# A last layer's loads moved from ScalarE's queue to SyncE's, and filler products tied to the statistics

## The chip, the cores and the metric

The kernel runs on one core of one Trainium2 chip. It is written in a tile framework in which a planner orders most instructions by its own costs and inserts the waits; in blocks marked as a manual schedule, the instructions of the named engines (of all engines, if none is named) keep the order in which they are written. The metric is device time in microseconds. Three runs of the kernel before took 3638.68, 3646.11 and 3650.18 us; the median is 3646.11.

## The reference

A tensor of 48 channels and 256 x 256 pixels passes through two layers, each with a residual. Layer 0 is an attention over 4 x 4 patches; layer 1 multiplies 64 x 64 windows by small matrices over width, height and channels. Cut to what matters:

```python
def _gn(v, G=16, eps=1e-5):            # group norm: 16 groups of 3 channels
    ...
    return ((g - m) / jnp.sqrt(s + eps)).reshape(v.shape)

def _L0_conv_ref(x, w_qkv, w_dw, temperature, w_proj):
    qkv = dwconv3x3(jnp.einsum('bchw,oc->bohw', x, w_qkv), w_dw)
    ...                                # heads, patches with a border, l2 norm
    attn = jax.nn.softmax(jnp.einsum('bhcn,bhcm->bhnm', q, k) * temperature, axis=-1)
    out = jnp.einsum('bhcn,bhnm->bhcm', v, attn)
    ...
    return jnp.einsum('bchw,oc->bohw', fold(out), w_proj)

def _L1_conv_ref(x, Ws, Hs, Cs, window_size):
    xb = x.reshape(B, C, H // ws, ws, W // ws, ws)
    return jnp.einsum('bcphqw,twW,thH,tcC->bCpHqW', xb, Ws, Hs, Cs).reshape(B, C, H, W)

x = x + _L0_conv_ref(_gn(x), ...)
x = x + _L1_conv_ref(_gn(x), Ws, Hs, Cs, 64)
```

## The kernel before

Layer 0 fills the first 3235 us and isn't touched. What follows is in two parts.

**Projection and statistics (L771 to L856).** Sixteen rows of pixels at a time, for both halves of the image, TensorE multiplies the attention's output by the projection (pps, L796), VectorE adds it to the pixels (L803) and takes the statistics of each 512 of them (bn_stats into st1, L807: 64 entries), and GpSimd stores the sum to x1s in DRAM (L812). The last step is done in two parts of 8 rows. SyncE then loads the first five pieces of x1s (L813 to L815). group_stats (L127) turns st1 into a mean and a reciprocal root in a short ping-pong between VectorE, TensorE and ScalarE, and the result is folded into the channel matrix csn (L849 to L855). In this block TensorE alone has a manual order: occupy(7) puts seven products without use ahead of the chain (identity by a tile nmx of zeros or row maxima, 256 columns, into a PSUM tile busy that nobody reads), and one more behind each small product of the chain.

**The last layer (L859 to L1014).** Its units are the 4 x 2 window rows and halves: yw is one of four bands of 64 image rows, xh the left or right 128 columns. For each unit over_c multiplies 32 rows of both window halves by csn (pa, L916), in 12 groups (4 pieces of 8 rows, each in groups of 3, 3 and 2 rows), and copies each group into zt (lzt, L924 to L928): VectorE mostly, ScalarE one group in four (one in two in the first unit). zt is laid out with the row index innermost, so that a copy in the order of pa steps 64 elements (256 bytes) at each element. over_w (pb, L942) multiplies by the width matrices, once for each of three t, and ScalarE copies the result into parts (lyt, L949). over_h (pc, L961) multiplies by the height matrices and sums over t; residual adds x1 (lrt, L975) and GpSimd stores to the output (L982). pa has two PSUM buffers, pb and pc one each; lyt and lzt have two SBUF buffers each.

**The order.** This part has a manual schedule on all engines. Unit u's over_w and over_h are interleaved with unit u + 1's over_c: for each of three channel groups q and each t, one over_w, then for t < 2 two groups of the next over_c, then, for t = 2, the over_h of the q before.

**The loads.** The inputs of later units come from x1s: rows (load_rows, L872, 64 x 4 rows of 1 KB, for the residual) and pieces (load_piece, L766, 48 channels x 4 rows, 4 KB runs, for over_c). rows_later and piece_later only put them in a list; begin_load (L899) takes the first of the list and issues it, after each over_w and each over_c group. They are issued from ScalarE's queue, which also holds ScalarE's copies, in program order. There are 44 of each kind.

Of the kernel before, what the change touches and what calls it, by code (L numbers as in the profile page):

```python
# [20 lines left out]
KS = 4  # L21
# [24 lines left out]
def conv_preact_kernel(  # L46
# [719 lines left out]
    def load_piece(yw, i, s, y, n, eng):  # L766

        y0 = yw * WS + s * HW + i * PR + y
        eng.dma_start(out=piece(yw, i)[s * 64 : s * 64 + C, y : y + n, :], in_=x1s[:, y0 : y0 + n, :])

    with tc.tile_pool(name="pj", bufs=3) as pj, tc.tile_pool(name="pjs", bufs=1) as pjs, tc.tile_pool(  # L771
        name="pps", bufs=3, space=PSUM
    ) as pps, tc.tile_pool(name="pp1", bufs=1, space=PSUM) as pp1:
        st1 = pjs.tile([P2, HALF * W // 512, 6], F32, name="st1")
        ov = os_.rearrange("t (c k) n -> t c k n", k=KK)
        for t in range(HALF // RP):
            ot = pj.tile([P2, KK, NP], F32, name="pot")
            xt = xts[t] if t < NX else pj.tile([P2, RP, W], F32, name="pxt")
            for s in range(2):
                r = slice(s * C, (s + 1) * C)  # L780
                y0 = s * HALF + t * RP
                nc.sync.dma_start(out=ot[r], in_=ov[s * (NT // 2 // TP) + t])
                if t >= NX:
                    nc.sync.dma_start(out=xt[r], in_=xc[:, y0 : y0 + RP, :])

            np = 2 if t + 1 == HALF // RP else 1
            R = RP // np
            for part in range(np):
                ys = slice(part * R, (part + 1) * R)
                n = R // KS * PX  # L790
                xv = xt[:, ys].rearrange("p (py ki) (px kj) -> p ki kj py px", ki=KS, kj=KS)
                for ki in range(KS):
                    ps = pps.tile([P2, KS, n], F32, name="pps")
# [24 lines left out]
        nc.gpsimd.memset(csn, 0.0)  # L818
        for s in range(2):
            nc.scalar.dma_start(  # L820
                out=csn[s * 64 : s * 64 + C].rearrange("c (t d) -> c t d", t=T3), in_=Cs.rearrange("t c d -> c t d")
            )
        at = pjs.tile([C, 64 + CK], F32, name="at")
        nc.gpsimd.memset(at, 0.0)
        for o in (C, 64 + C):
            nc.gpsimd.memset(at[:, o : o + 1], 1.0)
        gm2 = pjs.tile([P2, 64 + CK], F32, name="gm2")
        nc.vector.memset(gm2, 0.0)
        for o in (0, 64):
            nc.vector.tensor_copy(gm2[:, o : o + C], gm[:, 0:C])  # L830
        busy = pps.tile([P2, KS, 128], F32, name="pps")

        def occupy(n):

            for _ in range(n):
                nc.tensor.matmul(busy[:, 0:2, :], lhsT=ident[:, :P2], rhs=nmx, start=True, stop=True)

        with tc.manual_schedule(engines={mybir.EngineType.PE}):
            occupy(7)
            mv1, e1 = group_stats(st1, mean1, rstd1, pjs, pp1, lambda: occupy(1))  # L840
            pc1 = pp1.tile([64 + CK, 1], F32, name="pc1", tag="pstat")
            nc.tensor.matmul(pc1, lhsT=gm2, rhs=e1, start=True, stop=True)
            occupy(1)
            rstd2 = pjs.tile([64 + CK, 1], F32, name="rstd2")
            nc.vector.tensor_scalar_add(rstd2, pc1, EPS)
            nc.scalar.activation(rstd2, rstd2, AF.Sqrt)
            nc.vector.reciprocal(rstd2, rstd2)

            nc.vector.tensor_scalar_mul(csn, csn, rstd2)  # L849
            mcol = pjs.tile([C, 64 + CK], F32, name="mcol")  # L850
            nc.vector.tensor_scalar_mul(mcol, at, mean1[0:C])
            pb1 = pp1.tile([64 + CK, T3 * C], F32, name="pb1")
            nc.tensor.matmul(pb1, lhsT=mcol, rhs=csn[0:C], start=True, stop=True)
            occupy(1)
            nc.vector.tensor_sub(csn, csn, pb1)  # L855
    early.close()  # L856

# [1 line left out]
    with tc.tile_pool(name="lz", bufs=2) as lz, tc.tile_pool(name="lr", bufs=6) as lr, tc.tile_pool(name="ly", bufs=2) as ly, tc.tile_pool(name="ps1", bufs=2, space=PSUM) as ps1, tc.tile_pool(  # L859
# [20 lines left out]
            )  # L880

        loads = []

        def rows_later(yw, q):

            if yw < H // WS:
                for s in range(2):
                    for c in (0, 4):
                        loads.append(lambda s=s, c=c: load_rows(yw, q, s, c, 4, nc.scalar))

        def piece_later(n):

            yw, i = divmod(n, NPC)
            if yw < H // WS:
                for s in range(2):
                    for y in range(0, PR, PR // 2):
                        loads.append(lambda s=s, y=y: load_piece(yw, i, s, y, PR // 2, nc.scalar))

        def begin_load():  # L899

            if loads:
                loads.pop(0)()

        def over_c(u):

            yw, xh = units[u]
            zt = zts[u] = lz.tile([128, T3 * C, WS], F32, name="lzt")
            zv = zt.rearrange("p k (s y) -> p s y k", s=2)
            for p in range(NPC):
                xq = piece(yw, p)  # L910
                for g, (y0, n) in enumerate(((0, 3), (3, 3), (6, 2))):
                    pa = ps1.tile([128, 2, 512], F32, name="pa")
                    for i in range(n):
                        for s in range(2):
                            r = slice(s * 64, s * 64 + CK)
                            nc.tensor.matmul(  # L916
                                pa[:, s, i * T3 * C : (i + 1) * T3 * C],
                                lhsT=xq[r, y0 + i, xh * 128 : (xh + 1) * 128],
                                rhs=csn[r],
                                start=True,  # L920
                                stop=True,
                            )
                    y = p * PR + y0
                    to, src = zv[:, :, y : y + n, :], pa[:, :, : n * T3 * C].rearrange("p s (y k) -> p s y k", y=n)  # L924
                    if (p * 3 + g) % (4 if u else 2) == 1:
                        nc.scalar.copy(to, src)
                    else:
                        nc.vector.tensor_copy(to, src)  # L928
                    if xh and g == 2:
                        piece_later(yw * NPC + p + len(pieces))  # L930
                    yield

        def over_w(u, q, t):

# [54 lines left out]
        with tc.manual_schedule():  # L989
# [7 lines left out]
            for u in range(NU):  # L997
                yw, xh = units[u]
                ahead = over_c(u + 1) if u + 1 < NU else iter(())
                for q in range(NQ):  # L1000
                    if xh == 1:
                        rows_later(yw + 1, q)
                    parts[u, q] = ly.tile([128, T3, 1024], F32, name="lyt")
                    for t in range(T3):
                        over_w(u, q, t)
                        begin_load()
                        if t < 2:
                            for _ in range(2):
                                next(ahead, None)
                                begin_load()  # L1010
                        elif late:
                            over_h(*late)
                    late = u, q
# [42 lines left out]
```

## Time and profile before

| quantity | value |
|---|---|
| median of 3 runs | 3646.11 us (3638.68 to 3650.18) |
| the profiled execution | 3654.33 us, span 3652.5 us |
| TensorE products, busy | 3426.0 us (94%) |
| VectorE, ScalarE, GpSimd busy | 2115.9, 1898.0, 531.6 us |
| mean granted TensorE clock | 0.974 |
| first product of the last layer (pa) | 3380.54 us |
| last residual add | 3644.59 us |

PE is TensorE, PEld its weight loads, DVE VectorE, ACT ScalarE, POOL GpSimd, SP SyncE; ACTq and SPq are the queues of an engine where it issues transfers. A line of the timeline gives start, duration, engine, code line and operation, and in brackets how long the engine had been idle and what ended that. Matrix products of float32 run in two passes, so one product is two records. A line of stretches gives the busy time of each engine in the stretch, then TensorE's granted clock as a share of full speed, the DMA engines' busy share, and GB/s.

### The profile page before, as it was taken

To read this page: it belongs to the slowest core of one execution; us is meant where nothing else is said; L and a number is where in the kernel's file an instruction comes from. 1 tells how busy PE (TensorE), PEld (TensorE's weight loads), DVE (VectorE), ACT (ScalarE), POOL (GpSimd) and SP (SyncE) were. 2 spreads that over 40 slices of the span, in tenths; PEclk is the share of its full clock that TensorE was granted. 3 is DMA by queue.
4 is the path that set the end of the run, shared out by engine and by line. 5 is a ranking of instruction groups with operands and counts; after the bars stand their busy time and mean duration, and the time that the engine had idled before them with its cause. 6 is when DMAs were issued, how large, how long until landed. Compare 5 with 4: busy or idle time off the path is not lost.

```text
span 3652.5 us, 104961 instructions
## 1 busy us (share of the span) xinstructions
PE 3426.0 (94%) x46578; PEld 2874.1 (79%) x46578; DVE 2115.9 (58%) x3505; ACT 1898.0 (52%) x2699; POOL 531.6 (15%) x616
## 2 busy tenths in 40 slices
PE   2878999999999999999999999999999999976888
PEld 1337777888888888889888888888889888842765
DVE  5464775269727962796289528952894222257454
ACT  0245666566646664665466546654665444410343
POOL 2030121012201220122112111211121100010001
PEclk9988999999999999999999999999999999987899
DMA  7455665533323332333233323332333221059564
GB/s 159 157 125 146 169 183 154 172 92 97 91 74 87 95 86 74 86 93 94 73 82 98 90 81 82 93 86 81 82 93 92 62 54 28 19 141 283 119 156 107
DMA packets 241972, 386.78 MB, mean 106 GB/s; under 512 B 78130, under 2 KB 175778, under 8 KB 237000
## 3 DMA queue, kind: packets, MB, share of 16 engines
q1 hardware_dynamic: 187974, 244.77, 24.0%
q0 software_dynamic: 35264, 106.40, 12.8%
q10 hardware_dynamic: 18274, 28.83, 3.4%
q8 instruction: 368, 6.03, 0.7%
q14 instruction: 92, 0.75, 0.1%
HBM read 234.76 MB, written 144.90 MB: 104 GB/s over the span
## 4 chain that ended last, share of the span: by engine, by line
PE 81%; DMA 4%; DVE 3%; issue 2%; ACT 1%; SPq 1%; ACTq 0%; POOL 0%; POOLq 0%; DVEq 0%
PE big L339 37%; PE big L603 36%; PE pc L961 2%; PE pb L942 2%; PE pa L916 2%; PE big L179 1%; DVE acc L230 1%; PE pt L620 1%; DMA pxt<-in_x_dram 1%; DMA pad<-t 1%; PE pn L249 1%; DMA xs<-in_x_dram 1%; PE pst L557 1%; DVE xt L803 1%; DVE lzt L928 0%
## 5 line engine op out<-in xcount | busy, mean ns | idle before, releaser
L574 ACT ACTIVATE e<-big,nmx 128x1024 f32<-128x1024 f32 x1024 | 1143.9, 1117 | 878.0 <-PE big L339 617.8
L339 PE MATMUL big<-kt,qt 128*128 128x512 f32 x6144 | 1439.9, 393 | 31.9 <-DMA qt<-qkv 21.7
L603 PEld LDWEIGHTS big<-vn,e 128*64 128x64 f32 x32768 | 1358.7, 137 | 57.1 <-ACT e L574 30.6
L603 PE MATMUL big<-vn,e 128*64 128x96 f32 x32768 | 1389.1, 247 | 5.9 <-DVE oacc L614 2.4
L339 PEld LDWEIGHTS big<-kt,qt 128*128 128x128 f32 x6144 | 1148.4, 189 | 279.2 <-issue 29.3
L614 DVE TENSOR_TENSOR oacc<-big,oacc 128x768 f32<-128x768 f32 x480 | 453.4, 954 | 703.7 <-PE big L603 703.7
L230 DVE SCALAR_TENSOR_TENSOR acc<-pad,dwt,acc 126x1024 f32<-126x1024 f32 x592 | 765.6, 1293 | 39.7 <-ACT acc L211 23.9
L587 DVE TENSOR_REDUCE zt<-zs 128x1 f32<-128x4 f32 x256 | 38.5, 150 | 338.7 <-ACT e L574 338.7
L297 POOL DMA_DIRECT2D qkv<-o x72 | 52.8, 734 | 1247.6 <-ACT o L281 1247.6
L291 POOL TENSOR_TENSOR ol<-o,oh 126x1024 fp32r<-126x1024 f32 x78 | 184.7, 2368 | 311.7 <-DVE ss L245 238.4
L574 ACT ACTIVATION_READ_ACCUMULATOR e<-big,nmx 128x1 f32 x1024 | 196.2, 192 | 0.0
L281 ACT COPY o<-acc 126x1024 f32<-126x1024 f32 x74 | 158.8, 2146 | 0.0
L928 DVE COPY lzt<-pa 128x864 f32<-128x864 f32 (+1 forms) x69 | 101.2, 1507 | 69.2 <-PE pa L916 69.2
L949 ACT COPY lyt<-pb 128x1024 f32<-128x1024 f32 x69 | 70.7, 1025 | 116.3 <-PE pb L942 96.9
L241 ACT ACTIVATE sq<-acc 126x1024 f32<-126x1024 f32 x74 | 78.2, 1057 | 101.2 <-DVE acc L230 101.2
L796 PE MATMUL pps<-pot,wp 96*96 96x512 f32 x128 | 77.5, 770 | 56.2 <-DMA pot<-os__70 45.1
L182 ACT ACTIVATE ot<-big,bias 108x1024 f32<-108x1024 f32 x64 | 68.3, 1111 | 113.5 <-PE big L179 76.4
L211 ACT ACTIVATE acc<-pad,dwt 126x1024 f32<-126x1024 f32 x74 | 84.1, 1137 | 81.9 <-DMA pad<-t 81.9
L245 DVE TENSOR_REDUCE ss<-sq 126x64 f32<-126x1024 f32 x80 | 97.5, 1219 | 27.0 <-ACT sq L241 27.0
L942 PEld LDWEIGHTS pb<-wsb,lzt 64*64 64x64 f32 x4608 | 82.2, 140 | 37.2 <-issue 23.4
L219 PE MATMUL dps<-pad,diag 126*126 126x512 f32 x216 | 96.3, 606 | 15.5 <-DMA pad<-t 15.5
L796 PEld LDWEIGHTS pps<-pot,wp 96*96 96x96 f32 x128 | 26.0, 212 | 107.0 <-issue 73.8
(134 smaller groups left out, 2006.8 us busy)
## 6 DMA issues: line engine op xcount, KB each, us to landing
pad<-t SPq DMA_DIRECT2D x238, 254.0 KB
t<-ot SPq DMA_DIRECT2D x128, 217.7 KB
qkv<-ol POOLq DMA_DIRECT2D x78, 336.0 KB, 6.5
qkv<-oh POOLq DMA_DIRECT2D x70, 336.0 KB, 5.7
qt<-qkv SPq DMA_DIRECT2D x176, 96.0 KB
xs<-in_x_dram SPq DMA_DIRECT2D x128, 96.0 KB
os__70<-oo POOLq DMA_DIRECT2D x128, 96.0 KB, 2.1
pot<-os__70 SPq DMA_DIRECT2D x16, 768.0 KB
```

The source lines that it names most:

```text
L219: nc.tensor.matmul(ps[:, i, :], lhsT=diag[:, tap, :], rhs=self.pad[:, y : y + 2, dx : dx + W], start=(tap == 0), stop=(tap == 8),)
L230: nc.vector.scalar_tensor_tensor(self.acc, self.pad[:, dy : dy + KS, dx : dx + W], dwt[:, self.h, tap : tap + 1], self.acc, ALU.mult, ALU.add,
L245: nc.vector.tensor_reduce(self.ss, self.sq.rearrange("p a (x b) -> p x a b", b=KS), AX.XY, ALU.add)
L281: nc.scalar.copy(self.o.rearrange("p (a b) x -> p a b x", a=KS), self.acc.rearrange("p a (x b) -> p a b x", b=KS))
L291: eng.tensor_sub(self.ol, self.o, self.oh.bitcast(F32))
L339: nc.tensor.matmul(ps[:, i, :], lhsT=qt[:, r, q0 : q0 + 128], rhs=kts[2 * j + i][:, r // 2, :], start=(r == 0), stop=(r == 2),)
L574: nc.scalar.activation(e[:, j * 1024 : (j + 1) * 1024], ps.rearrange("p a b -> p (a b)"), AF.Exp, bias=nmx[:, b : b + 1], accum_out=zs[:, ...
L603: nc.tensor.matmul(ps[p : p + 64, j // 4, j % 4 * HD : (j % 4 + 1) * HD], lhsT=e[:, mb * 128 + p : mb * 128 + p + 64], rhs=vn, start=(i == 0),
L614: nc.vector.tensor_add(oaccs[h, k], ps[:, :, : 4 * HD], oaccs[h, k])
L796: nc.tensor.matmul(ps[:, i : i + step, :], lhsT=wp, rhs=ot[:, ki * KS + i : ki * KS + i + step, part * n : (part + 1) * n], start=True, st ...
L928: nc.vector.tensor_copy(to, src)
L942: nc.tensor.matmul(pb[s * WS : (s + 1) * WS, w, n * WS : (n + 1) * WS], lhsT=zts[u][r, t * C + b * 24 + q * 8 + s * 4 + i, :], rhs=wsb[r, ...
```

## The change

Four edits, all after the projection.

1. The seven filler products ahead of the statistics are replaced by eight that read what the statistics wait for: four read the last pixels, one for each of the four row sets ki that one VectorE add finishes, and four read st1, up to its 61st, 62nd, 63rd and 64th entry. Each therefore waits for the VectorE instruction that writes what it reads. The single products behind each step of the chain stay as they are.
2. The loads of the last layer (rows and pieces in the list) are issued from SyncE in place of ScalarE.
3. Ahead of each load SyncE issues a store of one float (4 bytes) to a scratch line in DRAM (turns). It reads an element that the step just before has written: of parts after an over_w, of zt after an over_c group. SyncE thus waits for that copy before it issues the store, and then the load. Nothing reads turns.
4. ScalarE's copies of pa into zt run through the elements in another order: for each k the 3 (or 2) rows y. They then write 3 (or 2) neighbours and step 576 bytes in PSUM. VectorE's copies stay as they are.

```diff
-        def occupy(n):
-            for _ in range(n):
-                nc.tensor.matmul(busy[:, 0:2, :], lhsT=ident[:, :P2], rhs=nmx, start=True, stop=True)
+        def occupy(rhs):
+            n = rhs.free_size()
+            nc.tensor.matmul(
+                busy.rearrange("p k n -> p (k n)")[:, :n], lhsT=ident[: rhs.shape[0], :P2], rhs=rhs, start=True, stop=True
+            )
 
         with tc.manual_schedule(engines={mybir.EngineType.PE}):
-            occupy(7)
-            mv1, e1 = group_stats(st1, mean1, rstd1, pjs, pp1, lambda: occupy(1))
+            for ki in range(KS):
+                occupy(xt[:, ys.start + ki : ys.stop : KS, :])
+            for i in range(4):
+                occupy(st1[:, : HALF * W // 512 - 3 + i, :])
+            mv1, e1 = group_stats(st1, mean1, rstd1, pjs, pp1, lambda: occupy(nmx))
...
+        turns = dram.tile([1, 256], F32, name="turns")
+        taken = []
...
-                        loads.append(lambda s=s, c=c: load_rows(yw, q, s, c, 4, nc.scalar))
+                        loads.append(lambda s=s, c=c: load_rows(yw, q, s, c, 4, nc.sync))
...
-                        loads.append(lambda s=s, y=y: load_piece(yw, i, s, y, PR // 2, nc.scalar))
+                        loads.append(lambda s=s, y=y: load_piece(yw, i, s, y, PR // 2, nc.sync))
 
-        def begin_load():
+        def begin_load(behind):
 
-            if loads:
+            if loads and behind is not None:
+                n = len(taken)
+                taken.append(nc.sync.dma_start(out=turns[:, n : n + 1], in_=behind))
                 loads.pop(0)()
...
-                        nc.scalar.copy(to, src)
+                        nc.scalar.copy(to.rearrange("p s y k -> p s k y"), src.rearrange("p s y k -> p s k y"))
...
-                    yield
+                    yield zt[0:1, 0, y : y + 1]
...
                         over_w(u, q, t)
-                        begin_load()
+                        begin_load(parts[u, q][0:1, t, 0:1])
                         if t < 2:
                             for _ in range(2):
-                                next(ahead, None)
-                                begin_load()
+                                begin_load(next(ahead, None))
```

More of the change, by code (lines that the diff above doesn't have):

```diff
@@ L831, in conv_preact_kernel @@
         busy = pps.tile([P2, KS, 128], F32, name="pps")
-        def occupy(n):
-            for _ in range(n):
-                nc.tensor.matmul(busy[:, 0:2, :], lhsT=ident[:, :P2], rhs=nmx, start=True, stop=True)
-        with tc.manual_schedule(engines={mybir.EngineType.PE}):
-            occupy(7)
-            mv1, e1 = group_stats(st1, mean1, rstd1, pjs, pp1, lambda: occupy(1))
+        def occupy(rhs):
[3 more added lines that the diff above has]
+            )
+        with tc.manual_schedule(engines={mybir.EngineType.PE}):
+            for ki in range(KS):
[3 more added lines that the diff above has]
+            mv1, e1 = group_stats(st1, mean1, rstd1, pjs, pp1, lambda: occupy(nmx))
             pc1 = pp1.tile([64 + CK, 1], F32, name="pc1", tag="pstat")
             nc.tensor.matmul(pc1, lhsT=gm2, rhs=e1, start=True, stop=True)
-            occupy(1)
+            occupy(nmx)
             rstd2 = pjs.tile([64 + CK, 1], F32, name="rstd2")
@@ L853, in conv_preact_kernel @@
             nc.tensor.matmul(pb1, lhsT=mcol, rhs=csn[0:C], start=True, stop=True)
-            occupy(1)
+            occupy(nmx)
             nc.vector.tensor_sub(csn, csn, pb1)
```

## The prediction

> **What bounds the kernel now.** I read the page first, then the chain, waits and timeline of the last layer alone, then the stretches of 3.41 us. The change touches only what runs after about 3366 us, so nine tenths of the time can't move.
>
> ```profile
> span 3652.5 us, 104961 instructions
> ...
> PE 3426.0 (94%) x46578; PEld 2874.1 (79%) x46578; DVE 2115.9 (58%) x3505; ACT 1898.0 (52%) x2699; POOL 531.6 (15%) x616
> ...
> PEclk9988999999999999999999999999999999987899
> ```
>
> TensorE is the bound, and its clock dips twice: at the start and around slice 37, the seam between attention and the last layer. The chain between 3404 and 3646 us, by line:
>
> ```profile
> by line: PE pc L961 26.0%; PE pb L942 25.4%; PE pa L916 20.5%; issue 8.0%; DVE lzt L928 5.3%; ACT lyt L949 4.3%; ACT lzt L926 3.9%; ACTq L877 3.7%; DVE lrt L975 2.0%; ACTq L769 1.0%; ACTq L949 0.0%; DVEq L928 0.0%; ACTq L926 0.0%
> ```
>
> Of 242 us, 72% are products; 8% "issue" is TensorE standing inside a group of pb products for no shown reason; 4.7% (11.4 us) is ScalarE's queue handing out loads (ACTq, L877 and L769). One such place in the timeline:
>
> ```profile
> 3581.08 1.01 ACT L949 COPY lyt<-pb 128x1024 f32<-128x1024 f32 x1 [3.30 <-PE pb L942]
> 3581.23 3.40 ACTq L877 DMA_DIRECT2D lrt<-x1s  x2
> ...
> 3584.68 1.63 ACT L926 COPY lzt<-pa 128x864 f32<-128x864 f32 x1 [2.59 <-PE pa L916]
> 3584.70 2.07 ACTq L877 DMA_DIRECT2D lrt<-x1s  x1
> 3586.36 0.55 PEld L916 LDWEIGHTS pa<-csn,lxq 49*128 49x128 f32 x8 [2.15 <-ACT lzt L926]
> ...
> 3586.82 1.01 ACT L949 COPY lyt<-pb 128x1024 f32<-128x1024 f32 x1 [0.51 <-issue]
> ...
> 3587.88 1.80 PEld L942 LDWEIGHTS pb<-wsb,lzt 64*64 64x64 f32 x64 [0.98 <-ACT lyt L949]
> ```
>
> Two row loads hold ScalarE's queue for 3.40 us instead of the usual 2 x 0.58; GpSimd had begun storing two 512 KB tiles at 3580.86. The copy of pa was ready to start at 3582.4 and starts at 3584.68; both PSUM buffers of pa are then full, TensorE waits, and its clock falls (pb takes 1.80, elsewhere 1.02).
>
> Busy time by stretches of 3.41 us (PE, PEld, DVE, ACT, POOL, then the granted clock):
>
> ```profile
> 3345.07:3348.49 3.42, 1.80 (x5) 0.41 (x3) 3.42 (x3) 0.00 (x0) 0.00 (x0) 1.00 0.96 321
> 3362.14:3365.55 3.41, 3.41 (x6) 1.13 (x5) 3.25 (x5) 0.00 (x0) 1.01 (x2) 0.50 1.00 310
> 3365.55:3368.97 3.42, 2.78 (x8) 0.88 (x7) 3.42 (x5) 0.00 (x0) 0.00 (x0) 1.00 1.03 249
> ...
> 3372.38:3375.79 3.41, 0.84 (x4) 0.41 (x4) 2.92 (x6) 0.00 (x0) 0.00 (x0) 1.00 0.96 332
> 3375.79:3379.21 3.42, 3.34 (x10) 2.12 (x10) 0.86 (x6) 0.41 (x2) 0.00 (x0) 0.50 0.49 180
> 3396.27:3399.69 3.42, 3.31 (x27) 2.90 (x24) 1.15 (x1) 1.51 (x2) 0.00 (x0) 0.50 0.02 5
> ```
>
> On this grid the clock changes only at borders. A stretch that is full of 96-row products lifts it; 1.80 of such products keeps it; 0.84 loses it at 3375.79. Stretches full of the 49-row pa products (3396.27) don't lift it: it stays at half until 3406.5, when pb has begun. So all of the first over_c (3380.5 to 3402.7) runs cold.
>
> **What the Trainium skill says.** "TensorE: Matmul & The Clock Gate", Part 1: the clock is gated to half by a monitor with a free-running window of 3413 ns. The trace agrees to 0.1 us (3341.66, 3365.55, 3375.79, 3406.51 are whole multiples apart); the row dependence is my reading of the trace. "DMA: Bandwidth & Descriptors", Issuing engines are not separate DMA queues: all transfers run on the same 16 engines, another issuer saves only its sequencer's time. The trace agrees that this time is what hurts here. "SBUF — State Buffer", Door 1: lines of 16 bytes, a penalty for each access that changes line. The trace has the price:
>
> ```profile
> L281 ACT COPY o<-acc 126x1024 f32<-126x1024 f32 x74 | 158.8, 2146 | 0.0
> L926 ACT COPY lzt<-pa 128x864 f32<-128x864 f32 x18 | 29.8, 1658 | 27.8 <-PE pa L916 25.3 <-DVE lzt L928 1.4 <-DMA lxq<-x1s 1.2
> L281 ACT COPY o<-dps 126x1024 f32<-126x1024 f32 x6 | 6.1, 1012 | 13.6 <-DVE dps L276 10.3 <-issue 3.3
> ```
>
> A strided read of SBUF doubles a copy, the same read of PSUM doesn't; lzt<-pa writes each element 256 bytes from the last and costs 1.92 ns each against 0.99.
>
> **The change part by part.**
>
> *Loads off ScalarE.* 44 row and 44 piece loads leave its queue. TensorE's waits that follow a long ACTq in the timeline: 0.44 (at 3502.6), 0.71 and 0.74 (3523.3, 3524.8), 0.69 (3550.1), 0.76 (3565.4), 1.94 and 0.76 (3586.4, 3587.9); sum 6.0. The cold stretch 3587.41 to 3590.83 costs half of 3.41, 1.7. What is late next: at 3582.4 the copy would end at 3584.0, TensorE needs it at 3584.4, so nothing; elsewhere pa's own copy is 0 to 0.3 behind. I take 7.5 of 7.7 (the chain's 11.4 includes issue that other work covers).
>
> *The same on SyncE.* After 3382.5 SyncE issues nothing in before. Now it issues 88 loads (0.31 a piece, 0.58 a row, from the ACTq rows) and 88 stores of 4 bytes, which no row shows: between 0.04 (a bare wait of ACTq) and 0.58. At 0.45 for all, 176 issues are 79 us of the 182 us in which loads are begun. Behind a waiting store on SyncE stand only later loads; who needs those? Pieces are read about half a unit (15 us) after their turn, rows about a unit (31 us). A load begins one copy (1.0 to 1.7) later than now. The slack covers it: 0. Without the cover it is microsecond for microsecond.
>
> *Waits for the stores' reads.* lyt and lzt may be overwritten only after the small store has read them. lyt is rewritten two q later, more than 10 us on; lzt a unit later. The extra waits sit on ScalarE and VectorE: some 3 per q and 4 to 8 per unit at 0.04, about 5 us in all, spread over engines that idle over 100 us in this layer. I take 0.5 on the path.
>
> *ScalarE's pa copy in the other order.* Reads 576 bytes apart in PSUM (o<-dps: no penalty at 16 bytes apart), writes in runs of 3 or 2. Bounds: 864 x 0.83 + 0.19 = 0.91 us (slope and offset of the lyt copy, 1.01 for 1024), and 2.6 (today's 1.66 plus the read penalty of o<-acc over o<-dps, 1.13 for 1024). I take 1.1. In the cold over_c the waits on ScalarE are 0.27 + 0.27 and the 1.22 before the first pb, of which 0.4 goes; later some 0.3 at 3431, 3461 and 3617. VectorE's copies keep 1.68 and bound the pairs. Credit 1.5; at the other end a loss of some 6 (0.9 on each of six copies of the first over_c, the later ones mostly covered by pb and pc).
>
> *Products.* Before: 7 products run from 3368.53 to 3371.8, then 3.0 us of nothing until 3374.79. Now four of 512 columns, each behind its add (adds end 3367.6 to 3370.4), two passes of 0.43 (the warm spacing of L796), 0.85 each: 3368.65 to 3372.1; then four of 366 to 384 columns at 0.31, each behind its statistics (the last at 3372.82): done at 3373.2, with 1.6 us to spare before the first use of TensorE, so no delay. The idle gap shrinks to 1.6, the stretch that lost the clock would hold 0.84 + 0.84. That is at the border (1.80 kept it, 1.72 at 3328 lost it), and the grid's place differs between executions. If it holds, four repeated products and pb1 run at double speed, 1.8 us on the chain between 3374.8 and 3380.5, and a stretch of pa is warm, 0.9. Then pa alone loses the clock: at about 2.6 us a pair it fills two thirds of a stretch, and one with 24 pa and 19 pb passes (3529.39) lost it. Bounds: a loss of 2.3 (if TensorE is cold at 3368.65, its products end that much after 3374.8) to a gain of 10. I take the clock as held through the statistics and one stretch: 2.7.
>
> Sum: 7.5 - 0.5 + 1.5 + 2.7 = 11.2. The profiled execution took 3654.33 (span 3652.5 and 1.8 around it), so it would take 3643. It is 8.2 over the median of the runs shown and above their highest; I carry the same difference to the median: 3646.1 - 11.2 = 3635. A measurement here tells about 0.3% (11 us) from nothing, so the forecast lies at that border.
>
> **Rivals.**
> *Hidden anyway (3643).* TensorE, freed of ScalarE, runs into its "issue" stands (11.3 us in this layer, often 1.1 to 1.8 at a time) or VectorE's copies. For: they are larger together than ACTq. Against: they stand beside the listed gaps, not under them. If they eat two thirds, 3.5 is left.
> *The clock holds (3627).* If pa alone keeps it, a pair costs 0.87 + 1.63 + 0.15 = 2.65 instead of 3.7 (22.2 / 6): 6.3 more, and with the waits after it 8. For: 1.80 of 3.41 has kept it. Against: stretch 3529.39.
> *SyncE falls behind (3656, slower).* Under GpSimd's stores one row load took 2.0 us to issue. Were that SyncE's mean in odd units, 24 issues take 48 us of 31; after the 10 us slack of lyt, ScalarE stops 7 us in each of three odd units: 21, on top of 3635. It decides from a mean of about 1.0 us per issue (32 issues in 31 us). Against: SyncE issued loads in 0.42 while the engines were full (3261 to 3290).
> *It doesn't do what it says:* the loads' order in time is set by the same copies; if the stores were not waited for, only the 1 us delay is gone.
>
> **How the numbers follow.** Forecast 0.52 (gains of 7 to 17, three fifths of it over 11, as waits under 0.3 us were left out of the sum), hidden 0.22, clock 0.14, behind 0.12. Faster 0.31 + 0.14 = 0.45; slower 0.12; same 0.43. The likeliest case alone is 3629 to 3639. For 8 in 10 I reach past the clock's case to its better end with the copy at 0.91 (3619), and through "hidden" to a small loss (the copy at 2.6, late products: 3650).
>
> **What would show it.** ACT has no DMA rows in the last layer, and the gaps after 3500 are gone; lzt on ScalarE near 1.1; clock 1.0 past the end of the statistics, half again soon after pa starts; SyncE under 0.6 per issue; no wait of lyt or lzt on a transfer. Wrong if ACT waits for SyncE's stores, if the copy is slower than 1.66, or if "issue" grows by what ACTq loses.

## The result, and the profile after

The changed kernel takes 3622.56 us (median of six runs, 3614.34 to 3629.20) against 3644.28 us of the kernel before (six runs, 3638.68 to 3652.45). The ratio is 0.9939, with a 95% interval of 0.992 to 0.9959. The gain is 21.7 us where 11.2 were forecast.

The profiled execution took 3626.91 us. Its page answers to the lines shown of before:

```profile
span 3625.1 us, 105190 instructions
...
PE 3407.1 (94%) x46580; PEld 2860.1 (79%) x46580; DVE 2115.9 (58%) x3505; ACT 1882.8 (52%) x2699; POOL 530.8 (15%) x616
...
PEclk9989999999999999999999999999999999987899
```

Product time fell by 18.9 us (3426.0 to 3407.1) with one product more (two records): mostly the same products at a higher clock. The rest of the 27.4 us between the two spans is time in which TensorE no longer stood. The trace says in which stage:

| stage | before | after |
|---|---|---|
| end of the last pixel add | 3370.44 | 3373.47 |
| from there to the first pa product | 10.10 | 8.54 |
| to the first pb product | 22.16 | 16.90 |
| to the last residual add | 241.89 | 218.25 |
| to the end of the span | 7.92 | 7.95 |

The first row is work that the change doesn't touch. In the fourteen profiles of this study it lies anywhere between 3362.55 and 3375.65, a spread about as wide as that of a kernel's six runs. So two profiles are compared from the last add on, and differences of a few us between kernels only by the runs' ratios. From the last add on, this pair differs by 30.4 us, more than the runs' 21.7: the profiled execution of before was a long one (3654.33 us against a median of 3644 to 3646).

The chain of the last layer's loop, 3398 to 3618 us, by line:

```profile
by line: PE pb L951 27.2%; PE pc L970 27.1%; PE pa L925 24.6%; DVE lzt L937 10.4%; DMA turns<-lzt 3.4%; issue 3.2%; ACT lyt L958 1.9%; DVE lrt L984 1.7%; ACT lzt L935 0.3%; SPq L882 0.3%; SPq L910 0.1%; DVEq L937 0.1%; ACTq L958 0.0%
```

Products are 79% of it (72% before), ScalarE's queue is gone, and "issue" fell from 8.0% to 3.2%. What TensorE waited for in the loop, first in the kernel before (3404 to 3646 us; total, times, longest):

```profile
PE pb L942 <- issue: 11.3, 13, 1.8
PE pb L942 <- ACT lyt L949: 3.9, 6, 1.1
PE pa L916 <- ACT lzt L926: 3.8, 4, 1.9
```

and after (3398 to 3618 us):

```profile
PE pb L951 <- issue: 4.2, 6, 1.0
PE pa L925 <- DVE lzt L937: 2.5, 8, 0.6
PE pb L951 <- ACT lyt L958: 1.4, 2, 1.1
```

The waits for ScalarE fell from 7.7 to 1.4 us, as the prediction meant them to (the wait of the first pb product for ScalarE's copy, 1.2 us before and 0.9 after, is left out of both). The stands called "issue" fell too, from 11.3 to 4.2; the prediction had left them as they were. They are the half of the result that has to be explained.

The copies of pa in the loop after, by shape (busy us, mean ns; idle before and what ended it):

```profile
L937 DVE COPY lzt<-pa 128x864 f32<-128x864 f32 x46 | 77.1, 1700 | 40.1 <-PE pa L925 38.4 <-ACT lyt L958 1.0 <-DMA turns<-lzt 0.7
...
L935 ACT COPY lzt<-pa 128x864 f32<-128x864 f32 x18 | 19.1, 1063 | 19.1 <-PE pa L925 19.0
L935 ACT COPY lzt<-pa 128x576 f32<-128x576 f32 x9 | 6.7, 750 | 6.2 <-PE pa L925 6.2
```

ScalarE's copy went from 1658 to 1063 ns; 1.1 us was forecast. The first line has the only wait of a copy for a small store: 0.7 us. The 3.4% "DMA turns<-lzt" of the chain above is this same store; "The rivals" below says why it is worth less.

The seam, by stretches of 3.41 us (PE, PEld, DVE, ACT, POOL, then the granted clock, DMA share and GB/s):

```profile
3377.89:3381.31 3.42, 2.68 (x15) 1.51 (x15) 1.46 (x9) 0.41 (x2) 0.00 (x0) 1.00 0.65 240
...
3384.72:3388.13 3.41, 2.12 (x30) 1.90 (x32) 1.42 (x1) 1.49 (x2) 0.00 (x0) 1.00 1.04 202
3388.13:3391.55 3.42, 2.39 (x36) 1.96 (x34) 1.88 (x2) 1.29 (x2) 0.00 (x0) 1.00 0.84 143
3391.55:3394.96 3.41, 2.00 (x30) 1.57 (x26) 2.55 (x2) 1.28 (x2) 0.00 (x0) 1.00 0.03 5
3394.96:3398.37 3.41, 2.77 (x20) 2.42 (x20) 1.50 (x2) 1.02 (x2) 0.00 (x0) 0.53 0.00 0
```

The clock is full through the statistics, as forecast, and stays full through 13 us of pa products alone, where one stretch was forecast. Stretches with 2.12 and 2.39 us of pa products keep it; after the next it goes to half. The 0.53 of the last line shows that these stretches lie a little ahead of the change, which comes at 3395.13; counted in stretches that end there, the last four of the full clock held 2.37, 2.14, 2.38 and 1.83 us. Busy time alone doesn't draw the border: in two of the experiments below the clock was lost after stretches of 2.14 (copy order alone) and 2.12 us (changed, old order).

### The profile page after: what moved, and what is told of

Read it like the earlier page. It is cut to its first block, busy times and chain, and to the rows that moved or that the text cites. A ratio compares the mean times of both kernels' runs of the same rounds, so it can differ in the third digit from the quotient of the medians.

```text
span 3625.1 us, 105190 instructions
## 1 busy us (share of the span) xinstructions
PE 3407.1 (94%) x46580; PEld 2860.1 (79%) x46580; DVE 2115.9 (58%) x3505; ACT 1882.8 (52%) x2699; POOL 530.8 (15%) x616
## 4 chain that ended last, share of the span: by engine, by line
PE 82%; DMA 4%; DVE 4%; issue 1%; ACT 1%; SPq 0%; POOL 0%; ACTq 0%; POOLq 0%; DVEq 0%
PE big L339 37%; PE big L603 36%; PE pa L925 2%; PE pb L951 2%; PE pc L970 2%; DVE acc L230 1%; PE big L179 1%; DMA pxt<-in_x_dram 1%; DVE lzt L937 1%; PE pt L620 1%; DMA pad<-t 1%; PE pn L249 1%; DVE xt L803 1%; PE pst L557 1%; DMA kt<-qkv 1%
## 5 line engine op out<-in xcount | busy, mean ns | idle before, releaser
L339 PE MATMUL big<-kt,qt 128*128 128x512 f32 x6144 | 1435.1, 392 | 33.6 <-DMA kt<-qkv 30.4
L313 POOL DMA_DIRECT2D kt<-qkv x44 | 22.9, 547 | 528.2 <-PE big L339 516.4
```

The costliest lines, as they stand in the source:

```text
L339: nc.tensor.matmul(ps[:, i, :], lhsT=qt[:, r, q0 : q0 + 128], rhs=kts[2 * j + i][:, r // 2, :], start=(r == 0), stop=(r == 2),)
```

## What the "issue" stands are

The page of both kernels has a transfer queue that the prediction did not look at (packets, MB, share of the engines):

```profile
q8 instruction: 368, 6.03, 0.7%
```

These are 368 packets of 16,384 bytes. TensorE executes 93,970 instructions in the kernel before, weight loads and semaphores counted; 93,970 / 256 is 367. The Trainium skill, "Runtime: NRT & Kernel Launch", Instruction fetch mechanics, says the same of an engine's instructions: they come in blocks of 16 KiB, 256 instructions, over a transfer queue of the engine's own, while the block before is executed. It calls the cost "mostly hidden". In the attention it is: between 1000 and 3150 us TensorE has no pause over 0.15 us at all. In the last layer it isn't. I numbered TensorE's instructions by their starts, 256 to a block, and set each block beside its packet:

```
before, us         previous   fetch      landed     TensorE's stand
block              began      began
327                3437.48    3440.77    3442.18    3442.16 - 3443.79
329                3448.29    3452.03    3453.28    3453.29 - 3454.71
333                3468.47    3472.61    3473.49    3473.57 - 3475.03
344                3524.97    3528.63    3529.96    3530.39 - 3531.51
```

In these four a stand ends 1.4 to 1.6 us after its block has landed. The fetch takes 1.1 us on the mean. What differs is how long after the start of the block before it begins: 0.9 us at the best, 2.8 on the mean of the last layer, over 3 us in 23 of its 48 blocks. In the attention a block lasts 8 us, and this doesn't matter. In the last layer a block lasts 4.9 us (median), and 3 + 1.1 + 1.5 is more than that. After the change the mean is 2.2 us, with 9 of 48 blocks over 3 us, though a block now lasts only 4.5 us. Counting the pauses over 0.15 us that end 1.2 to 1.8 us after a block's landing, before has 15.1 us of them in the last layer (18 pauses, of 28.5 us of pauses in all) and after has 6.0 (8 pauses, of 16.5). This is called "late blocks" below. It is a rough measure, since a pause with another cause can end within that distance too: with the landings shifted at random against the pauses, 3.1 us would on the mean be counted before and 1.4 after (an estimate from these two traces).

What stood ahead of block 327? The timeline of before:

```profile
3436.73 0.94 ACTq L769 DMA_DIRECT2D lxq<-x1s  x2
...
3438.31 0.31 ACTq L769 DMA_DIRECT2D lxq<-x1s  x1
...
3439.70 0.59 ACTq L877 DMA_DIRECT2D lrt<-x1s  x1
...
3440.33 2.25 ACTq L877 DMA_DIRECT2D lrt<-x1s  x2
...
3441.01 1.14 PE L942 MATMUL pb<-wsb,lzt 64*64 64x64 f32 x58
3443.79 0.28 PE L942 MATMUL pb<-wsb,lzt 64*64 64x64 f32 x3 [1.64 <-issue]
```

Six loads of 192 and 256 KB in under 6 us, in groups, since ScalarE issues a load for a VectorE copy too without waiting for that copy. After, SyncE's queue at a like place:

```profile
3439.94 0.21 SPq L910 DMA_DIRECT2D turns<-lyt  x1
3440.20 0.58 SPq L882 DMA_DIRECT2D lrt<-x1s  x1
...
3441.55 0.21 SPq L910 DMA_DIRECT2D turns<-lzt  x1
3441.82 0.58 SPq L882 DMA_DIRECT2D lrt<-x1s  x1
```

One load at a time, each behind its store. That the packets tell when a block came is a reading of the trace; that the bunching of loads is what makes blocks late is what the experiments had to show.

## The experiments

Times are medians; ratios are to the kernel before, run beside each, with 95% intervals. "pa stage" is from the first pa to the first pb product, "loop" from there to the last residual add, "late" the late blocks up to that add, all of the one profiled execution. That execution was the fastest of its kernel's runs for "copy order alone", "changed, old order" and "changed, loads bunched", so their stages are better than their times.

| kernel | time | ratio | pa stage | loop | late |
|---|---|---|---|---|---|
| before | 3644 to 3646 | 1 | 22.2 | 241.9 | 15.1 |
| products alone | 3646.6 | 1.0002 (0.9992 to 1.0012) | 23.4 | 237.5 | 15.5 |
| copy order alone | 3648.6 | 1.0000 (0.9989 to 1.0012) | 20.3 | 231.7 | 13.3 |
| products and order | 3638.0 | 0.9988 (0.9977 to 0.9999) | 15.8 | 233.4 | 14.4 |
| loads on SyncE, small stores | 3635.4 | 0.9964 (0.9951 to 0.9977) | 22.2 | 220.8 | 7.2 |
| loads on SyncE, bare | 3661.9 | 1.0048 (1.0035 to 1.0060) | 22.2 | 248.4 | 25.3 |
| changed, old products | 3630.6 | 0.9960 (0.9944 to 0.9975) | 20.9 | 223.4 | 7.6 |
| changed, old order | 3629.6 | 0.9966 (0.9948 to 0.9983) | 19.0 | 219.4 | 5.2 |
| changed | 3622.6 | 0.9939 (0.9920 to 0.9959) | 16.9 | 218.3 | 6.0 |
| changed, loads bunched | 3637.6 | 0.9978 (0.9967 to 0.9989) | 16.9 | 224.8 | 10.1 |
| before, small stores on ScalarE | 3689.2 | 1.0110 (1.0091 to 1.0129) | 19.7 | 279.6 | 7.5 |
| changed, VectorE's order too | 3623.4 | 0.9940 (0.9917 to 0.9964) | 17.0 | 219.6 | 10.2 |
| changed, halved row loads | 3622.4 | 0.9930 (0.9914 to 0.9946) | 16.9 | 219.6 | 8.2 |
| both of these | 3620.6 | 0.9926 (0.9907 to 0.9946) | 17.7 | 220.8 | 9.4 |

### Each edit alone

The theory was that of the prediction: most of the gain is ScalarE's issue time, the other edits add a few us each.

*The products alone* (edit 1; the rest as before):

```diff
...
-            occupy(7)
+            for ki in range(KS):
+                occupy(xt[:, ys.start + ki : ys.stop : KS, :])
+            for i in range(4):
+                occupy(st1[:, : HALF * W // 512 - 3 + i, :])
...
```

> Edit 1 alone: the fillers that read the last pixels and st1; the loads and copies stay as before. My theory: the clock is held through the statistics and some stretches of pa, so the first pa starts 1.6 us sooner after the last adds, and pa to the first pb takes less than before's 22.2 us, but each pair of groups is still bound by a copy of 1.66: some 19. The loop behind it (first pb to last residual add, 241.9 before) is untouched. Sum 4 to 5 us, ratio 0.9987. Rival (the loop's gain of the changed kernel comes from a warm clock in its first part): the loop is shorter by more than 5 us here too, ratio under 0.9975.

Measured: 1.0002. The clock is lost at 3376.5, 3.4 us after pa has begun, and the pa stage is no shorter. Nor do the products shorten the way from the last add to pa by themselves: that takes between 8.54 and 10.1 us without them and between 8.53 and 11.6 with them in the fourteen profiles.

*ScalarE's copy order alone* (edit 4):

```diff
-                        nc.scalar.copy(to, src)
+                        nc.scalar.copy(to.rearrange("p s y k -> p s k y"), src.rearrange("p s y k -> p s k y"))
```

> Edit 4 alone: ScalarE's copies of pa in the other order. Theory: they take 1.06 us as in the changed kernel; the first over_c gets 0.9 us shorter, and in the loop TensorE's waits on ScalarE shrink by 2, the stands named issue stay near 11 us on pb. 2 to 4 us in all, ratio 0.999. Rival (a shorter copy frees ScalarE enough to absorb the load issue, so ScalarE's queue was harmless once its copies are short): the loop is shorter by 8 us or more, ratio 0.9975.

Measured: 1.0000, though the copies take the new, shorter time (962 ns on the mean over both sizes, against 1534).

*The loads on SyncE with their small stores* (edits 2 and 3):

```diff
-                        loads.append(lambda s=s, c=c: load_rows(yw, q, s, c, 4, nc.scalar))
+                        loads.append(lambda s=s, c=c: load_rows(yw, q, s, c, 4, nc.sync))
...
-            if loads:
+            if loads and behind is not None:
+                n = len(taken)
+                taken.append(nc.sync.dma_start(out=turns[:, n : n + 1], in_=behind))
                 loads.pop(0)()
...
```

> Edits 2 and 3 alone: loads on SyncE, each behind its 4 byte store. Theory: the waits behind ScalarE's queue go (7.5 us) and the stands named issue fall to some 4 us as in the changed kernel (another 9): 14 to 17 us, ratio 0.9958. Rival (the stands shrink because of the other two edits): only the 7.5 us, ratio 0.998, stands of 10 us or more on pb.

Measured: 0.9964, 13 us. TensorE's waits in its loop (3408.5 to 3646 us):

```profile
PE pb L946 <- issue: 4.6, 6, 1.3
PE pa L920 <- DVE lzt L932: 3.3, 8, 0.5
PE pb L946 <- ACT lyt L953: 1.4, 2, 1.1
```

Waits for ScalarE fell from 7.7 to 1.4 us, late blocks from 15.1 to 7.2: 6.3 + 7.9 = 14.2, and waits for VectorE's copies grew by 1.4 (from 1.9). That is the size of the measured 13.

*The loads on SyncE without the stores* (edit 2 alone; a load is then begun as soon as its buffer is free):

```diff
...
-                        loads.append(lambda s=s, y=y: load_piece(yw, i, s, y, PR // 2, nc.scalar))
+                        loads.append(lambda s=s, y=y: load_piece(yw, i, s, y, PR // 2, nc.sync))
```

> Edit 2 without edit 3: loads on SyncE, no small stores, so each load starts as soon as its buffer is free and the rest of the list's order is kept. Theory (bursts of loads delay what TensorE fetches, the small stores spread them): ScalarE's waits go (7.5 us), but the stands named issue stay at 10 us or more, and more of them fall early in the unit where the loads bunch: ratio 0.998. Rival (the stands come from ScalarE's queue, pacing is worth nothing): the same as with the stores, ratio 0.996, stands under 5 us.

Both expectations missed, and on the other side: 1.0048, 16 us slower than before and 26 slower than with the stores. ScalarE issues nothing here either. Its timeline shows what the stores had been keeping apart:

```profile
3424.01 3.37 SPq L769 DMA_DIRECT2D lxq<-x1s  x5
3427.43 11.04 SPq L877 DMA_DIRECT2D lrt<-x1s  x11
...
3437.07 1.23 PE L942 MATMUL pb<-wsb,lzt 64*64 64x64 f32 x36 [4.01 <-issue]
```

Eleven row loads in one go. The fetches of TensorE's blocks 326 and 327 begin 7.4 and 11.7 us after the block before has begun; TensorE stands for 4.01 us until 1.46 after the first has landed, and for 3.35 us at the second. So taking the loads off ScalarE is not what decides. The theory from here on was that it is how many loads are under way together; its rival was that the gain is ScalarE's freedom alone.

### Are the blocks late because of bunched loads?

*The changed kernel with its loads bunched by three:*

```diff
-                loads.pop(0)()
+                for _ in range(min(count, len(loads))):
+                    loads.pop(0)()
...
-                        begin_load(parts[u, q][0:1, t, 0:1])
+                        begin_load(parts[u, q][0:1, t, 0:1], 3 if t < 2 else 1)
                         if t < 2:
                             for _ in range(2):
-                                begin_load(next(ahead, None))
+                                next(ahead, None)
```

> The changed kernel with its loads bunched: three loads behind one small store after each of the first two pb copies of a q, none behind the pa copies; the same loads, on the same SyncE, a third of the stores there. Theory A (TensorE's stands that the profile can put down to nothing, issue, come from loads that are begun together: 11.3 us before, 4.2 after, 20.9 with loads on SyncE and no stores): they return to 9 to 13 us, time 3628 to 3632, ratio 0.9955. Theory B (the gain is only that ScalarE no longer issues): stands and time as in the changed kernel, 3623, ratio 0.994.

Measured: 3637.6, 15 us above the changed kernel, so the bunching took back most of the gain, with ScalarE as free as there. Its queue and its waits:

```profile
3433.44 0.22 SPq L910 DMA_DIRECT2D turns<-lyt  x1
3433.71 2.97 SPq L882 DMA_DIRECT2D lrt<-x1s  x3
```

```profile
PE pb L952 <- issue: 7.2, 11, 1.4
PE pa L926 <- issue: 2.6, 2, 1.8
```

These stands called "issue" are 9.8 us together, within the 9 to 13 that the theory expected; the time is more than it expected, and far from the rival's. So ScalarE's freedom alone isn't the whole gain. How much of the 15 us is late blocks isn't shown. The profiled execution has 10.1 us of them, 4.1 more than the changed kernel's, but a profile of loads that aren't bunched, "VectorE's order too" further down, has 10.2. And it is the fastest of its 20 runs (3625.35, of up to 3649.4), so what the slow ones stood for isn't seen.

*The kernel before with the small stores on ScalarE's own queue* (edit 3 without edit 2):

```diff
...
+                taken.append(nc.scalar.dma_start(out=turns[:, n : n + 1], in_=behind))
                 loads.pop(0)()
...
```

> The kernel before, its loads still issued by ScalarE, but each behind a 4 byte store of what was just written, as the change has it on SyncE. Products and copy order as before. Theory A (the pacing alone is the gain: instruction blocks of TensorE come late behind loads that are begun together; 15.1 us of stands after such a block in the kernel before, 7.2 with paced loads on SyncE, 24.5 with bare loads on SyncE): stands of 6 to 9 us and 3633 to 3638, ratio 0.997, as the loads' edits on SyncE (3635.4). Theory B (pacing needs an engine that has nothing else to do: ScalarE stands in front of each small store until VectorE's copy is done, and the pb copies queue behind): stands also 6 to 9 us, but the pb products wait for ScalarE's copies by 10 us or more, 3645 to 3665, ratio 1.000 to 1.005.

(The 24.5 us count the bare loads' stands up to 3640 us; up to the last add they are the 25.3 of the table.)

Theory B, and worse than it said: 3689.2, 45 us slower. What ScalarE and then TensorE waited for (3400 to 3660 us):

```profile
ACT lyt L953 <- DMA turns<-lzt: 27.8, 18, 3.4
ACT lzt L930 <- DMA turns<-lzt: 17.9, 6, 3.7
```

```profile
PE pa L920 <- ACT lzt L930: 23.3, 16, 3.0
PE pb L946 <- ACT lyt L953: 21.9, 20, 3.4
PE pa L920 <- DVE lzt L932: 1.9, 8, 0.4
PE pb L946 <- issue: 1.1, 2, 0.7
```

45.7 us of ScalarE waiting at its small stores become 45.2 us of TensorE waiting for ScalarE. And the stands called "issue" are almost gone (1.1): fetches begin 1.8 us after the block before on the mean, and 4 of 48 over 3 us. (Of the 7.5 us that the table counts as late, 3.4 are one wait for ScalarE that happens to end 1.5 us after a landing.) So pacing makes the fetches timely on ScalarE too, but there TensorE pays for ScalarE's waits. Pacing and moving the loads are therefore one measure: each alone makes the kernel slower (by 45 and by 16 us), together faster by 13.

*Halved row loads in the changed kernel*, 128 KB, each behind its own store:

```diff
-                    for c in (0, 4):
-                        loads.append(lambda s=s, c=c: load_rows(yw, q, s, c, 4, nc.sync))
+                    for c in (0, 2, 4, 6):
+                        loads.append(lambda s=s, c=c: load_rows(yw, q, s, c, 2, nc.sync))
```

> The changed kernel with each load of rows in two halves, 128 KB each, each half behind its own small store: 40 loads in the 42 places of two units in place of 28. Theory A (a late instruction block is late by the bytes that stand in front of it): stands after a late block fall from 6.0 to 3 or 4 us, time 3618 to 3621, ratio 0.9935. Theory B (what is left of the stands comes from GpSimd's stores of 512 KB, which are as before): stands 5 to 7 us, time 3622 to 3625. Theory C (the loads now fill all places and come late): waits of pa on its rows or of the last adds on theirs, slower than 3628.

The time is the changed kernel's (3622.4). Theory A falls: late blocks did not shrink (8.2). B's time is met (its stands, 5 to 7 us, are not), but GpSimd's stores as the cause of what is left weren't tested. So what makes a fetch late, the number of loads, their bytes or the stores beside them, stays open.

### Why do the small edits count only in the end?

*The changed kernel with the old products, and with the old order* (edits 1 and 4 undone, one at a time; the diffs are the first two above, reversed).

> The changed kernel with the old products (36 of 96 rows of constants) in place of those that read the rows and the statistics; loads and ScalarE's copy order stay changed. Each of these two edits alone was worth nothing (1.0002 and 1.0000), yet the whole change is 12.8 us below the loads' edits alone (3622.6 against 3635.4). Theory A (the two need each other): the new products bring the stage of pa products to its start with a full clock, and the quicker copies make that stage dense enough to keep it. Without the products the clock is half through pa again: first pa to first pb about 22 us in place of 16.9, time 3628 to 3635, ratio to the unchanged kernel 0.996. Theory B (it is the copy order that became worth something once the loads left ScalarE): as the changed kernel, 3623, ratio 0.994.

> The changed kernel with ScalarE's copies in the old order (864 numbers in 1.66 us in place of 1.06); loads and products stay changed. Theory A (the two need each other): the clock is lost again soon after pa begins, as in the run of the products alone, first pa to first pb 22 us or more: 3630 to 3636, ratio 0.996 to 0.997, as the loads' edits alone. Theory B (the copy order alone became worth something): the same 3630 to 3636 in the end, but by waits of the pa and pb products on ScalarE's copies of 4 us or more, with the clock as in the changed kernel. Theory C (the products carry it): 3624, ratio 0.994.

The medians are 8 and 7 us above the changed kernel, half-way to the loads' edits alone; the ratios, 0.9960 and 0.9966, are those of the loads' edits alone (0.9964). With intervals of 0.3 to 0.4%, "each a little" and "both needed" can't be told apart by the times. The stage speaks more plainly: the pa stage is 20.9 and 19.0 us with one of the two edits and 16.9 with both. Theory A's mark, about 22, was too high for both. Its mechanism fits these two profiles: with the old products the clock was half from 3374 until pb had begun; with the old order it was lost at 3378, 5 us after pa's start.

Over all fourteen profiles it needs a correction. The old products don't always come too late. In two of the six kernels with them the clock was full at pa's start as well: for 3.3 us with the copy order alone and for 7.2 us with the small stores on ScalarE (first pa at 3378.79):

```profile
3378.70:3380.40 1.70, 1.64 (x25) 1.59 (x24) 0.50 (x1) 0.00 (x0) 0.00 (x0) 1.00 0.01 5
3383.80:3385.50 1.70, 1.53 (x24) 1.31 (x22) 0.13 (x1) 1.23 (x2) 0.00 (x0) 1.00 1.26 180
```

That kernel has neither of the two edits, and its pa stage is 19.7 us. With the new products the clock was full at pa's start in all eight, for 3.4 to 5.1 us with ScalarE's old copy order and for 5.8 to 13.1 with the new. So the new products make certain what was chance before, as far as fourteen executions can tell, and the quicker copies make it last.

*Both small edits, loads left on ScalarE* (edits 1 and 4):

> The kernel before with the new products and ScalarE's new copy order together, its loads left on ScalarE: the corner that is missing. Alone each was worth nothing there (1.0002 and 1.0000); with the loads on SyncE behind small stores the two together were worth 12.8 us (3635.4 to 3622.6) and each alone 5 to 6. Theory A (the gains are swallowed where the loads come bunched, since TensorE then waits for its late instruction blocks in any case): 3641 to 3646, ratio 0.999 to 1.000, stands after late blocks of 13 us or more. Theory B (the two are needed together, to carry the full clock into pa, and their gain has nothing to do with the loads): first pa to first pb about 17 us, 3632 to 3636, ratio 0.997.

Measured: 0.9988, 4 us (0 to 8). The pa stage is 15.8 us, as B had it, so the two edits carry the clock into pa whatever the loads do. By the ratio the time is nearer A; by the median, 3638.0, it lies between the two. The loop is 233.4 us with 14.4 us of late blocks, as in the other kernels that load from ScalarE without stores (13.3 to 15.5). The loads' edits have a ratio of 0.9964 and the whole change 0.9939, which makes the two edits worth 9 us with an uncertainty as large. 4 and 9 agree within it: that bunched loads swallow part of their gain is possible and not shown.

### VectorE's copies

*VectorE's copies of pa in the new order as well*, in the changed kernel and in that with halved loads:

```diff
-                        nc.vector.tensor_copy(to, src)
+                        nc.vector.tensor_copy(to.rearrange("p s y k -> p s k y"), src.rearrange("p s y k -> p s k y"))
```

> The changed kernel with VectorE's copies of pa in the order that ScalarE's have now. VectorE's copies hold 10.4% of the chain of waits in the loop of the last layer, some 23 us in 65 copies of 1.70 and 1.18 us. Theory A (the order of the addresses in SBUF costs VectorE as it cost ScalarE, 1658 to 1063 ns): 864 numbers in about 1.1 us, a third of those 23 us goes, time 3614 to 3618, ratio 0.992. Theory B (VectorE's time is set by its number of elements, not by their order): still 1.70 us, time 3623, ratio 0.994; then ScalarE should have more of the copies.

> The changed kernel with halved loads of rows and with VectorE's copies in ScalarE's new order. The order alone took VectorE's copies from 1.70 to 1.13 us and left the time where it was (3623.4), with stands of 10.2 us after late instruction blocks in its profile (6.0 in the changed kernel's). Theory A (its gain went into stands, and halved loads give it back): 3612 to 3617, ratio 0.992. Theory B (VectorE's copies held up TensorE by only some 2.5 us in all, so there was nothing to gain): as with halved loads alone, within 2 us.

VectorE's copy does fall, to 1132 ns, and the time doesn't move: 3623.4, and 3620.6 with halved loads against 3622.4 without the order. The row and the chain of the first:

```profile
L937 DVE COPY lzt<-pa 128x864 f32<-128x864 f32 x41 | 45.8, 1132 | 39.4 <-PE pa L925 38.0 <-DMA turns<-lyt 1.3
```

```profile
by line: PE pb L951 35.2%; PE pa L925 30.1%; PE pc L970 28.3%; issue 4.3%; ACT lyt L958 1.4%; DVE lrt L984 1.1%; ACT lzt L935 0.3%; ACTq L958 0.0%
```

The 10.4% of VectorE are gone from the chain, and pb and pa have taken them over, 27.2 to 35.2% and 24.6 to 30.1%. The chain had gone through VectorE's copies while TensorE was just as busy beside them. What TensorE really waited for VectorE was 2.5 us in the loop, the line of the waits shown above; that was the bound on this gain. No version tried is measurably better than the changed kernel.

## Why the prediction was right and where it was wrong

The direction and the range held (3635 forecast, 3619 to 3650; 3622.6 measured); the gain was twice the forecast. 3622.6 lies outside the 3629 to 3639 of the case held likeliest. The range held because it had been stretched for a clock that holds, while some 8 us of the gain came from stands that the prediction had left as they were: that is in part luck. By the steps:

*Loads off ScalarE, 7.5.* The mechanism was right and is the term that was mis-sized. Edits 2 and 3 are worth 13 us (8 to 18 by the interval). The waits for ScalarE, listed at 6.0 us in the forecast, fell by 6.3. What it had no term for is 8 us of late instruction blocks (15.1 to 7.2 in the two profiles). The step that failed is the one that left the 11.3 us of "issue" as they are, "for no shown reason". A reason was to be had: several of the long stands lie 256 or 512 product records apart, each record with its weight load, and the page has an instruction queue.

*The same on SyncE, 0.* SyncE's slack was judged rightly: its small store takes 0.21 us (0.40 when queued), a row 0.58, and the mean of all its issues there is 0.47 against the 0.45 taken. What it waited for in the loop after were the copies, as planned:

```profile
SPq L910 <- ACT lyt L958: 50.4, 20, 13.0
SPq L910 <- DVE lzt L937: 28.0, 17, 5.3
```

But the step asked only whether the loads come too late. That they come apart is the larger effect: 26 us between the loads on SyncE with stores and without. In the fourth rival stood the sentence "if the stores were not waited for, only the 1 us delay is gone"; the bare loads show it to be wrong by more than the whole gain.

*Waits for the stores' reads, -0.5.* About right: 0.7 us, once, on VectorE.

*ScalarE's copy order, 1.5, and the products, 2.7.* The copy's price was right (1.06 us for 1.1). Together they gave 4 us with the loads on ScalarE and some 9 with an equal uncertainty in the changed kernel, so 4.2 can't be called wrong. The split was: alone each is worth nothing that can be measured. The products' 1.8 us in the statistics didn't come; the way from the last add to pa varies as much with them as without. Their worth is the full clock at pa's start, and it needs the denser pa to last.

*The rivals.* "Hidden anyway" is refuted: the stands shrank instead of eating the gain. "The clock holds" is half true: full clock for 13 of the 16.9 us of the pa stage in this profile, and for 5.8 to 12.9 us in the five others with both edits, where it was given 0.14. Its counter-argument, one stretch that lost the clock with 24 pa and 19 pb passes, held of that density only: 30 pa passes that were busy for 2.12 of 3.41 us kept it. "SyncE falls behind" shows at five of the 88 small stores, which took 1.2 to 2.1 us to issue instead of 0.21. A copy waited behind one of them: the store of 3503.61 landed 7.41 us after its start, and VectorE's copy waited 0.68 us for it. The chain goes through these 7.41 us, but the copy could have started only 0.68 us sooner, so that is the most that it can have cost. "It doesn't do what it says" is refuted by the timeline.

## What to carry to other kernels

Ask of a transfer not only who issues it and whether it comes in time, but how many are under way at once. An engine's program comes by transfers too: here TensorE used up a block of 256 instructions in about 5 us, and stood for 4.0 us when the fetch of the next one began late, beside the bare loads. Loads that aren't urgent can be spread by making each wait for a step of the work, on a queue on which nobody waits; on a queue that others need the same wait was a loss (45 us here). And read a gain from what the bounding engine waits for, not from another engine's share of the chain: VectorE's copies held 10.4% of it, and the next path was as long.

## What was not expected of the hardware

- TensorE's instructions arrive in 368 packets of 16 KiB; in the last layer many stands end about 1.5 us after such a packet lands, and a block's fetch began from under 1 to 11.7 us after the block before it had begun.
- In the changed kernel a full clock was kept by stretches of 49-row pa products that were busy 2.14 and 2.38 of 3.41 us and lost after one of 1.83, while stretches full of such products (3.31) didn't lift a half clock before. In other runs it was lost after 2.12 and 2.14.
- A copy on VectorE that writes runs of 3 in SBUF and reads PSUM 576 bytes apart takes 1132 ns for 864 numbers, against 1700 with single writes 256 bytes apart; on ScalarE it is 1063 against 1658.
